# A convolution and state-space stack: the last projection through memory, the gate begun amid the last convolution, scans made up bit by bit, step sizes in one projection

## The chip, the cores and the metric

The kernel runs on one core of one Trainium2 chip. A core has five engines with a queue of instructions each: TensorE (PE in the profile, its weight loads PEld) multiplies matrices, VectorE (DVE) and ScalarE (ACT) work elementwise, GpSimd (POOL) does elementwise work too, and SyncE (SP) here only issues DMAs. An engine runs its queue in order; queues wait for each other by semaphores. Data lies in the chip's SBUF, results of matmuls in PSUM, everything larger in memory behind DMAs. The metric is the device time of one execution in microseconds (us); lower is better.

## The reference

Eight images of 256 channels and 32 x 32 places pass through four layers, each on the group norm `_gn` of its input and added to it:

```python
x = x + L0(_gn(x))   # attention, 8 heads of 64, queries and keys normalized to length 1, times 10
x = x + L1(_gn(x))   # 3x3 convolution 256 -> 256, weights = sign * scale
x = x + L2(_gn(x))   # 3x3 convolution 256 -> 256
x = x + L3(_gn(x))   # the mixer below
```

The mixer sees an image as 1024 places (N) of 256 channels:

```python
xn = layernorm(xs)                                   # over channels
for each of 4 blocks of 64 channels (mamba):
    u, z = split(xc @ inw.T); u = silu(conv4(u))     # 128 inner channels
    xdbc = u @ xpw.T                                 # 4 + 16 + 16 columns
    dt = softplus(xdbc[..., :4] @ dtw.T + dtb);  Bm, Cm = xdbc[..., 4:20], xdbc[..., 20:]
    h_t = exp(dt_t * A) * h_(t-1) + dt_t * u_t * Bm_t ;  y_t = sum over 16 states of h_t * Cm_t + u_t * D
    xm = (y * silu(z)) @ outw.T + skip * xc
Q = qpw(qdw(x_concat));  xg = sigmoid(Q) * xm        # one gate per block and place
R = rpw(rdw(xg)) + xg                                # depthwise 3, then 256 -> 256
xm2 = fpw(fdw(cat(xs, R))) + xs                      # depthwise 3, then 512 -> 256
x_out = cat(lc(xm2), mha(xm2)) @ fc_w.T + fc_b       # depthwise 3 beside attention, 8 heads of 32
xi = gelu(layernorm(x_out)); xi = ln_hw(xi); xi = dwc 3x3 (xi)
out = layernorm(xi) @ proj_w.T + proj_b
```

All of it is fp32.

## The kernel before

**Stages.** A tile framework orders the instructions: the program issues them as Python generators run, a scheduler orders each engine's queue by priority, data and free buffers, and sets the semaphores. Stage b of eight runs three images side by side: the scans of image b (`scan_layers`, L1028), and a dense stream (`dense`, inside the main loop at the end of the function) with the rest of the mixer of image b-1 and layers 0 to 2 of image b+1. Ahead of stage 0 stand layers 0 to 2 of image 0, after stage 7 the back of image 7. In stage 0 the dense stream has only a front, in stage 7 only a back; stages 1 to 6 have all three.

**Pace.** `interleave` (L1449) runs the dense stream step by step. Each step names its cost, about the microseconds of its matmuls; after each `pace` of cost the scans get one step of 149. `PACE` is 1.8 for stage 0, 2.95 for stages 1 to 6, 1.6 for stage 7. A dense stream with a lull gives a cost of 0 for some steps and pays what it owes with the next step (`lull`); `slow` takes a share of 0.35 of the front attention's cost. A scan instruction may not be moved ahead of the dense instruction issued before it on its engine (`Paced`, L97).

**Order of a dense stream.** In stages 1 to 6:

1. `back_layers` of b-1 (L1193): qdw and qpr (the gate: a convolution over 3 places and a 4 x 4 product as matmuls, tanh on ScalarE, two multiplications on VectorE), loads of xs (the mixer's input, kept in memory as xd), depthwise rd, projection rpw, depthwise fd (4 tiles), projection fpw, then `mixer_attention`: v, q/k, 64 units of scores, exp and values (tiles qk, p, acc; results o3), during which the depthwise `local` tiles and the next image's statistics are made (step 56).
2. `front_attention` of b+1 (L598): four double blocks of v (w<-xn matmuls), then `pair(0)`, the q and k of the first two heads with their lengths.
3. `back_out` of b-1 (L1356): the last projection of attention and local tiles, `fc`, 16 matmuls; two results xo go to memory.
4. The rest of `front_attention`: 64 units of two heads each, with sums by VectorE.
5. `front_convs` (L772): projection wout, group norm, convolution 1 (72 matmuls of 512 columns), group norm, convolution 2. Amid its steps, at the places (5, 6, 8 ... 26), stands `back_end` of b-1 (L1374): xo is loaded, layer norm with gelu, `ln_hw`, the 3x3 depthwise convolution (dw, 16 VectorE ops), layer norm, projection projw, and the output.

**Scans.** A branch (block of 64 channels) has its input prepared in `branch_front` (L806): minw, a convolution over 4 places on VectorE (u), projection mxpw to 36 rows, of which 32 (B and C) go to memory and the last 4, copied with them by ScalarE into `low`, give the step sizes dt in a second matmul with K = 4 (mdtw). dt and dt * u (du) go to memory and come back with each row on 4 groups of partitions. `scan_steps` (L907) then has 16 units a branch, 64 an image: GpSimd multiplies du and B ("drive", L958), ScalarE makes the decays (da), VectorE runs two scans, GpSimd multiplies with C ("weigh", L990), and two matmuls a unit, y<-hs,sel, add up the states. `branch_back` closes the branch with z and moutw.

**Buffers that matter.** `work` tiles are 12 buffers of 128 x 1026; PSUM has two `big` tiles of 128 x 1024, one `acc`, two `da`, one `y`. Loads of scans, stores and round trips through memory go by SP's queue, weights by ScalarE's.

Of the kernel before, what the change touches and what calls it, by code (L numbers as in the profile page):

```python
# [19 lines left out]
P = 128  # L20
# [13 lines left out]
def preact_stack(ctx: ExitStack, tc: tile.TileContext, I, out, cols):  # L34
# [130 lines left out]
    mdtw = wp.tile([36, NB, P], F32, name="mdtw")  # L165
    nc.sync.dma_start(out=mdtw[32:36], in_=I["mdtw"])
# [75 lines left out]
    for t in images + [raw]:  # L242
        nc.gpsimd.memset(t, 0.0)

# [353 lines left out]
    def front_attention(src, img, exact=False):  # L598
# [11 lines left out]
        for kt in range(0, NKT, 2):  # L610
            ps = big_tile()
            for i in range(2):
                for c in range(2):
                    tensor.matmul(
                        ps[:, HALVES[i]],
                        xn[c][:, (kt + i) * P : (kt + i + 1) * P],
                        wv[c],
                        start=c == 0,
                        stop=c == 1,
                    )  # L620
            vector.tensor_copy(
                v[:, kt : kt + 2].rearrange("p a b -> p (a b)"), ps
            )
            yield 3.4
# [98 lines left out]

        if exact:
            attention_exact(heads())
        else:
            first = pair(0)
            yield 3.4
# [77 lines left out]
    def branch_front(i, xn, br):  # L806
# [34 lines left out]
        for h in range(2):  # L841
            ps = da_tile()
            tensor.matmul(
                ps[0:36], mxpw[:, i], u[:, HALVES[h]], start=True, stop=True
            )
            scalar.copy(low[0:36, HALVES[h]], ps[0:36])
# [12 lines left out]
        for h in range(2):  # L859
            ps = da_tile()  # L860
            tensor.matmul(
                ps, mdtw[32:36, i], low[32:36, HALVES[h]], start=True, stop=True
# [330 lines left out]
    def back_layers(img, exact=False, begin=None):  # L1193
# [52 lines left out]
        for t in range(2):  # L1246
            depthwise3(rd[t][:, 0:N], xm[t], "rdw_w", "rdw_b", t)

# [28 lines left out]

        local = []
# [6 lines left out]
        for n, cost in enumerate(mixer_attention(x2, img, exact)):  # L1285
# [3 lines left out]
            if n == 56 and begin is not None:  # L1289
                next(begin)  # L1290
        while len(local) < 2:
            add_local()
        img["mix"] = local
# [62 lines left out]
    def back_out(img):  # L1356

        local, o = img.pop("mix"), img.pop("o3")
        img["xo"] = xdp.tile([2, P, N], F32, tag="xo", name="xo_d")

        def evac_fc(m, ps):
            xo = work("xo")[:, 0:N]
            scalar.activation(xo, ps, AF.Identity, bias=fc_b[:, m : m + 1])
            nc.sync.dma_start(out=img["xo"][m], in_=xo)

        srcs = [t[:, 0:N] for t in local + o]
# [7 lines left out]
    def back_end(img, out_b):  # L1374
        xo = [work("xo")[:, 0:N] for _ in range(2)]
        for t in range(2):
# [284 lines left out]
```

## Time and profile before

| | us |
|---|---|
| median of 8 runs | 6522.96 |
| lowest and highest | 6516.68, 6534.22 |
| the profiled execution: time | 6528.06 |
| its span, first to last instruction | 6526.2 |
| TensorE busy | 5561.0 |
| VectorE busy | 4008.6 |
| GpSimd busy | 2721.6 |
| ScalarE busy | 2714.1 |
| granted TensorE clock, mean | 0.91 |

The profile has several views: busy time of each engine in the span and in 40 slices, busy time in chosen stretches, instructions in order of time with what each waited for, and waits added up by who waited for whom. In the timeline a line is a run of equal instructions: start, length, engine, operation, output<-inputs, form and count, then in brackets the idle time before it and what ended it. A matmul of 512 columns stands there as two records. Times inside the span are counted from its first instruction. The stages begin at about 383, 1019, 1786, 2564, 3336, 4106, 4868 and 5640 us; the back of the last image begins at 6209.

### The profile page before, as it was taken

How to read it: one execution, taken by the hardware profiler on the slowest of the kernel's cores; microseconds unless marked ns; L12 is line 12 of the kernel's file. 1: busy time of each engine (PE TensorE's matmuls, PEld its weight loads, DVE VectorE, ACT ScalarE, POOL GpSimd, SP SyncE). 2: the span in 40 equal slices, each digit the busy share in tenths (PEclk: the TensorE clock that was granted, in tenths of full speed). 3: DMA queues.
4: the chain of work that ended last, by engine and by line, in shares of the span. 5: the costliest groups of instructions: out<-in, count | busy, mean ns of one | idle time of the engine just before them, and what ended most of it. 6: DMA issues, size and time to landing. Idle time of an engine off the chain costs nothing.

```text
span 6526.2 us, 52241 instructions
## 1 busy us (share of the span) xinstructions
PE 5561.0 (85%) x17310; PEld 1882.1 (29%) x17310; DVE 4008.6 (61%) x4612; ACT 2714.1 (42%) x3253; POOL 2721.6 (42%) x1302
## 2 busy tenths in 40 slices
PE   8887688998889978989889988899889997877496
PEld 2331133223332233222332233322332223311232
DVE  4248846577556775567755766567756677545622
ACT  3224424553255533544336442455325543345242
POOL 0007653634535243542526436353444535266600
PEclk9988899999899989999899998999899998988697
DMA  1023232322233122321223222232223312233201
GB/s 42 26 63 82 73 94 71 91 67 72 79 90 87 45 80 78 104 78 48 78 79 95 78 58 82 83 92 59 78 83 86 91 46 76 69 98 95 79 26 37
DMA packets 220145, 479.21 MB, mean 73 GB/s; under 512 B 60500, under 2 KB 102100, under 8 KB 218840
## 3 DMA queue, kind: packets, MB, share of 16 engines
q1 hardware_dynamic: 163416, 402.34, 21.8%
q10 hardware_dynamic: 56448, 73.43, 3.9%
q8 instruction: 139, 2.28, 0.2%
q14 instruction: 142, 1.16, 0.1%
HBM read 402.70 MB, written 64.49 MB: 72 GB/s over the span
## 4 chain that ended last, share of the span: by engine, by line
PE 49%; DVE 24%; ACT 7%; DMA 7%; issue 6%; POOL 5%; SPq 1%; ACTq 0%; DVEq 0%; POOLq 0%
PE big L105 30%; PE acc L105 11%; DVE hs L105 7%; PE da L105 6%; DVE p L105 4%; POOL hs L990 4%; PE y L105 3%; DVE dw L105 2%; ACT p L105 2%; ACT da L105 2%; DVE u L105 2%; DMA dt<-dt_m 1%; DVE dt L105 1%; POOL hs L958 1%; DMA bc<-bc 1%
## 5 line engine op out<-in xcount | busy, mean ns | idle before, releaser
L958 POOL TENSOR_TENSOR hs<-du,bc 128x1024 f32<-128x1024 f32 x512 | 1345.5, 2648 | 1620.7 <-DMA du<-du_m 1102.8
L990 POOL TENSOR_TENSOR hs<-hs,bc 128x1024 f32<-128x1024 f32 x512 | 1299.0, 2538 | 1004.6 <-DVE hs L105 846.0
L105 ACT ACTIVATE p<-big 128x1024 f32<-128x1024 f32 x1024 | 1038.9, 1021 | 734.1 <-PE big L105 725.7
L105 PE MATMUL acc<-p,v 128*64 128x512 f32 x4096 | 1153.5, 635 | 17.2 <-ACT o L105 12.2
L105 ACT ACTIVATE da<-dt,a_neg 128x512 f32<-128x512 f32 x1024 | 685.1, 687 | 1064.0 <-DVE hs L105 473.2
L105 PE MATMUL big<-im,w 128*128 128x512 f32 x2304 | 1108.3, 635 | 14.7 <-ACT im L105 14.7
L105 DVE TENSOR_TENSOR p<-p 128x1024 f32<-128x1024 f32 x448 | 769.6, 1718 | 261.1 <-PE acc L105 122.1
L105 DVE TENSOR_TENSOR_SCAN hs<-da,carry,hs 128x512 f32<-128x512 f32 x512 | 621.9, 1264 | 278.3 <-ACT da L105 201.4
L105 DVE TENSOR_TENSOR_SCAN hs<-da,hs 128x512 f32<-128x512 f32 x512 | 600.5, 1210 | 247.7 <-ACT da L105 238.5
L105 PE MATMUL y<-hs,sel 128*32 128x512 f32 x2048 | 459.7, 680 | 284.4 <-POOL hs L990 283.5
L105 PE MATMUL big<-q,k 64*128 64x512 f32 x2048 | 628.5, 670 | 63.3 <-ACT p L105 27.0
L105 PE MATMUL big<-qk,qk 64*128 64x512 f32 x2048 | 626.4, 659 | 53.3 <-ACT p L105 41.6
L105 PEld LDWEIGHTS big<-im,w 128*128 128x128 f32 x2304 | 451.0, 202 | 693.8 <-issue 642.9
L105 PEld LDWEIGHTS acc<-p,v 128*64 128x64 f32 x4096 | 214.7, 138 | 825.8 <-issue 730.5
L989 POOL COPY carry<-hs 128x2 f32<-128x2 f32 x256 | 87.5, 342 | 863.6 <-DVE hs L105 748.4
L105 PEld LDWEIGHTS big<-qk,qk 64*128 64x128 f32 x2048 | 172.0, 191 | 489.6 <-issue 285.6
L105 PEld LDWEIGHTS big<-q,k 64*128 64x128 f32 x2048 | 171.0, 192 | 489.6 <-issue 271.2
L105 PE MATMUL big<-xn,w 128*128 128x512 f32 x512 | 243.4, 631 | 28.0 <-DVE v L105 28.0
L105 DVE SCALAR_TENSOR_TENSOR dw<-xo,vec,dw 128x961 f32<-128x961 f32 (+1 forms) x128 | 243.2, 1945 | 29.6 <-ACT dw L105 29.1
L105 PEld LDWEIGHTS y<-hs,sel 128*32 128x32 f32 x2048 | 59.4, 113 | 594.0 <-POOL hs L990 438.9
L105 DVE SCALAR_TENSOR_TENSOR u<-raw,vec,u 128x1024 f32<-128x1024 f32 x96 | 162.4, 1691 | 84.9 <-ACT u L105 83.3
L105 PE MATMUL big<-o,w 128*128 128x512 f32 x384 | 181.2, 624 | 30.2 <-DVE o L105 30.2
(211 smaller groups left out, 5042.9 us busy)
## 6 DMA issues: line engine op xcount, KB each, us to landing
bc<-bc SPq DMA_DIRECT2D x1024, 128.0 KB
du<-du_m SPq DMA_DIRECT2D x512, 128.0 KB
dt<-dt_m SPq DMA_DIRECT2D x512, 128.0 KB
w<-in_wc ACTq DMA_DIRECT2D x192, 192.0 KB
rs<-inv SPq DMA_DIRECT2D x64, 256.0 KB
dt_m<-dt SPq DMA_DIRECT2D x64, 256.0 KB
du_m<-a SPq DMA_DIRECT2D x64, 256.0 KB
w<-in_wqk ACTq DMA_DIRECT2D x64, 128.0 KB
```

The lines of the kernel that those rows point to most:

```text
L105: made = issue(*args, **kwargs)
L958: nc.gpsimd.tensor_mul(u["hs"], u["du"], both_groups(u["bc"][:, 0]))
L989: nc.gpsimd.tensor_copy(carry[:, u["q"], g : g + 2], hs[:, :, HALF - 1])
L990: nc.gpsimd.tensor_mul(hs, hs, both_groups(u["bc"][:, 1]))
```

## The change

- **Last projection.** `back_layers` stores local and o3 (4 tiles of 512 KB) to memory at its end. `back_out` loads them and is no longer run before the front attention, but amid `front_convs`, after the wout projection's steps, ahead of `back_end`; its results xo stay in SBUF, so that their two stores and two loads go.
- **Front's start.** `pair(0)` is made after two of the four blocks of v.
- **Gate.** The first three steps of image b's own `back_layers` (`EARLY`: gate, and rd) run at the last places of stage b's `front_convs`, once the scans of image b are through; stage b+1 goes on from there. Stage 1 still begins its back afresh.
- **Scans.** `PACE` of stages 1 to 6 is 2.78 instead of 2.95. A lull's debt is paid with at most a quarter of each step's cost (`MAKE_UP`). With it the scans are issued to their end at a cost of 417 of 440 in a stage, where they ended with the last step before.
- **Step sizes.** At the start the two weights of the step sizes are multiplied into one of 128 x 128 a branch; dt comes from u in one matmul with K = 128. mxpw has 32 rows.

```diff
-    mdtw = wp.tile([36, NB, P], F32, name="mdtw")
-    nc.sync.dma_start(out=mdtw[32:36], in_=I["mdtw"])
+    mdtw = wp.tile([P, NB, P], F32, name="mdtw")
...
+    low_rank = work("low_rank")[0:DTR, 0:N].rearrange("r (k i n) -> r k i n", k=2, i=NB)
+    nc.sync.dma_start(out=low_rank[:, 0], in_=I["mxdt"])
+    nc.sync.dma_start(out=low_rank[:, 1], in_=I["mdtw"])
+    made = acc_tile()
+    for i in range(NB):
+        tensor.matmul(
+            made[:, i * P : (i + 1) * P],
+            low_rank[:, 0, i],
+            low_rank[:, 1, i],
+            start=True,
+            stop=True,
+        )
+    vector.tensor_scalar_mul(mdtw.rearrange("p i n -> p (i n)"), made, 0.5)
...
+        for kt in range(0, NKT, 2):
...
             yield 3.4
+            if kt == 2 and not exact:
+                first = pair(0)
+                yield 3.4
...
         else:
-            first = pair(0)
-            yield 3.4
             yield from attention(
...
-                ps[0:36], mxpw[:, i], u[:, HALVES[h]], start=True, stop=True
-            )
-            scalar.copy(low[0:36, HALVES[h]], ps[0:36])
+                ps[0 : 2 * DS], mxpw[:, i], u[:, HALVES[h]], start=True, stop=True
+            )
+            scalar.copy(low[0 : 2 * DS, HALVES[h]], ps[0 : 2 * DS])
...
-                ps, mdtw[32:36, i], low[32:36, HALVES[h]], start=True, stop=True
+                ps, mdtw[:, i], u[:, HALVES[h]], start=True, stop=True
...
             depthwise3(rd[t][:, 0:N], xm[t], "rdw_w", "rdw_b", t)
+        yield 0
...
+        img["mix"] = xdp.tile([4, P, N], F32, tag="mix", name="mix")
...
-            if n == 56 and begin is not None:
-                next(begin)
+            if n == 56 and "begin" in img:
+                next(img["begin"])
...
-        img["mix"] = local
+        for t, part in enumerate(local + img.pop("o3")):
+            nc.sync.dma_start(out=img["mix"][t], in_=part[:, 0:N])
...
-        local, o = img.pop("mix"), img.pop("o3")
-        img["xo"] = xdp.tile([2, P, N], F32, tag="xo", name="xo_d")
+        srcs = [work("mix")[:, 0:N] for _ in range(4)]
+        for t in range(4):
+            nc.sync.dma_start(out=srcs[t], in_=img["mix"][t])
+        yield 0
+        xo = img["xo"] = [work("xo")[:, 0:N] for _ in range(2)]

         def evac_fc(m, ps):
-            xo = work("xo")[:, 0:N]
-            scalar.activation(xo, ps, AF.Identity, bias=fc_b[:, m : m + 1])
-            nc.sync.dma_start(out=img["xo"][m], in_=xo)
-
-        srcs = [t[:, 0:N] for t in local + o]
+            scalar.activation(xo[m], ps, AF.Identity, bias=fc_b[:, m : m + 1])
...
-        xo = [work("xo")[:, 0:N] for _ in range(2)]
-        for t in range(2):
-            nc.sync.dma_start(out=xo[t], in_=img["xo"][t])
+        xo = img.pop("xo")
...
-                yield cost + owed
-                owed = 0.0
+                more = min(owed, MAKE_UP * cost)
+                owed -= more
+                yield cost + more
...
+    MAKE_UP = 0.25
+    PLACES = [1, 4, 4, 4, 4, 5, 6, 8, 9, 10, 11, 12, 13, 14, 15, 16]
+    PLACES += [18, 20, 22, 24, 26, 27, 28, 29]
+    EARLY = 3
-    PACE = [1.8] + [2.95] * (batch - 2) + [1.6]
+    PACE = [1.8] + [2.78] * (batch - 2) + [1.6]
...
-            for n, cost in enumerate(back_layers(last, begin=front)):
+            back, begun = last.pop("back", None), EARLY
+            if back is None:
+                back, begun = back_layers(last), 0
+            if front is not None:
+                last["begin"] = front
+            for n, cost in enumerate(back, begun):
                 yield cost
-                if n == 2 and front is not None:
+                if n == 3 and front is not None:
                     next(front)
+            ending = chain(back_out(last), back_end(last, out[b - 1]))
...
-            yield from islice(front, 4)
-            yield next(front)
-            yield from back_out(last)
+            yield from islice(front, 5)
             yield from slow(front)
+            imgs[b]["back"] = back_layers(imgs[b])
             yield from amid(
                 lull(front_convs(imgs[b + 1]), LULLS),
-                back_end(last, out[b - 1]),
-                (5, 6, 8, 9, 10, 11, 12, 13, 14, 15, 16, 18, 20, 22, 24, 26),
+                chain(ending, islice(imgs[b]["back"], EARLY)),
+                PLACES,
             )
```

## The prediction

> **What bounds the kernel now.** I read the page's busy shares and slices first, then the table of stages for one image, then TensorE's timeline and waits at the places where that table shows it idle. One profiled execution gives all durations. Its span is 6526.2 us and its time 6528.06, 5.1 us above the median 6522.96 of the eight runs, so the sum is made against 6528.06 and 5 us are taken off at the end. A difference under 0.2% (13 us) I count as no change.
>
> ```profile
> PE 5561.0 (85%) x17310; PEld 1882.1 (29%) x17310; DVE 4008.6 (61%) x4612; ACT 2714.1 (42%) x3253; POOL 2721.6 (42%) x1302
> PE   8887688998889978989889988899889997877496
> POOL 0007653634535243542526436353444535266600
> ```
>
> TensorE carries the span, at 85%; GpSimd, which drives and weighs the scans, falls to 2 or 3 tenths at each image's boundary. The steady stages (one image's back, the next one's front, a third one's scans) last 762 to 778 us. The stage from 4105 us, cut at its parts:
>
> ```profile
> 4105.00:4146.00 41.00, 31.00 (x101) 15.24 (x99) 30.06 (x73) 21.52 (x23) 0.00 (x0) 0.88 0.24 84
> 4183.00:4363.00 180.00, 165.56 (x628) 42.43 (x628) 102.78 (x95) 115.60 (x139) 113.43 (x58) 0.97 0.38 102
> 4396.00:4416.00 20.00, 16.58 (x48) 6.33 (x40) 16.35 (x25) 9.18 (x13) 5.70 (x3) 0.97 0.33 104
> 4416.00:4598.00 182.00, 172.50 (x628) 46.15 (x624) 140.34 (x140) 97.38 (x118) 61.46 (x24) 0.98 0.19 53
> 4621.00:4640.00 19.00, 13.52 (x50) 9.27 (x50) 15.30 (x33) 5.10 (x5) 7.17 (x4) 0.64 0.06 21
> 4640.00:4760.00 120.00, 95.86 (x220) 34.80 (x218) 97.86 (x101) 37.26 (x43) 65.41 (x29) 0.87 0.28 81
> ```
>
> Columns: length, then busy time of TensorE, its weight loads, VectorE, ScalarE and GpSimd, granted clock, DMA. The two attentions (lines 2 and 4) are TensorE's own time at nearly full clock. It loses at the boundaries: the back's start (line 1), after the first group norm's statistics (line 5, clock 0.64) and in the first convolution (line 6, VectorE 82% busy). Line 3 holds the last projection.
>
> ```profile
> 4386.30 9.39 PE L105 MATMUL big<-xn,w 128*128 128x512 f32 x16 [4.90 <-DVE v L105]
> 4396.62 7.13 PE L105 MATMUL big<-local,w 128*128 128x512 f32 x16
> 4403.59 7.03 PE L105 MATMUL big<-o,w 128*128 128x512 f32 x16
> 4415.03 1.92 PE L105 MATMUL y<-hs,sel 128*32 128x512 f32 x4 [3.42 <-POOL hs L990]
> 4416.88 1.76 PE L105 MATMUL big<-q,k 64*128 64x512 f32 x4
> 4624.57 0.39 PE L105 MATMUL acc<-mv,gmat 128*128 128x4 f32 x2 [3.44 <-DVE mv L105]
> 4627.36 6.99 PE L105 MATMUL acc<-mean_w,ln_sq 128*128 128x1 f32 x32
> 4639.45 7.40 PE L105 MATMUL big<-im,w 128*128 128x512 f32 x12
> ```
>
> A matmul of 512 columns is two records, 0.86 us. The last projection (32 records, 13.8 us) stands between the q/k projection and the front attention; from the last projection of attention to the first convolution matmul pass 18.3 us (4621.1 to 4639.4) with little to do.
>
> ```profile
> PE y L105 <- POOL hs L990: 30.6, 14, 4.4
> PE acc L105 <- DVE mv L105: 6.4, 2, 3.4
> ```
>
> The largest wait of this stage, 30.6 us in 14 pieces, is for weighed scan states; 19.4 us of it lie in 4640 to 4760, behind VectorE's depthwise convolution.
>
> **The change part by part**, in the order in which the changed program's engines hold their instructions.
>
> *Last projection out of the front's start.* Stages 1 to 6 each lose its 13.8 us there. From the back attention's last matmul group (4363.5) to the first score (4416.9) are 53.4 us. After the change: value blocks 0 and 1, q/k, value blocks 2 and 3, scores. The matmuls up to 4395.6 remain, with their 4.9 us wait (32 us). What is late next is the k chain: in image 0, where nothing covers it, 6.2 us pass between q/k and scores ("<-ACT k"). Two value blocks (6.9 us) now cover it, but VectorE copies them out behind the chain and one scan pair, about 3 us more. So 35.4 us, a gain of 18. Bounds: 20 (no wait) and 8 (copying the value blocks out holds the scores as long as the old projection's rest).
>
> *The projection behind the front's first group norm.* Its 13.8 us fill the 18.3 us there. It waits for its PSUM banks (two evacuations of 1.28 us with statistics between, about 2.5 us) and the statistics matmuls in its midst wait some 1.5 us; the scan matmuls and the step-size matmul (1.7 us) stay. The first convolution matmul comes about 3 us later than now. The layer norm's 32 small records, 7.0 us here at the low clock and 3.6 at full clock, move into the convolution: 3.6. Cost 6.6 instead of 13.8 + 3.6 = 17.4; bounds 0 and 17.4. On SP four stores of 512 KB replace two, and four loads two. The stores stand among scan loads near the back attention's end, the last behind the final multiplication of o3; behind it wait dt and bc loads, whose units have 6 to 23 us of slack there. The loads are issued where the two xo loads stand (4610.7); those two are read 7.8 and 9.9 us later, so at 2.1 us each the last of four lands at 4624.8, against a first use at 4621 and a last one 10 us after. Nothing, then; the cover gone, it would be the wait of the present xo reader, 14.4 us. At the end of the run the trip lies before the projection instead of after it (6.95 us from projection to squares now): 0, within 5 us.
>
> *First convolution.* VectorE gains the projection's time to work ahead on the scans, and the changed order puts three instead of four scan pairs inside the depthwise ops. I take 4 us of the 19.4 us of waits. Bounds: 15 gained, 9 lost (the eight units 40 to 47 now stand within 33 matmuls instead of 43: 8.6 us less cover). The made-up emission and pace 2.78 are in this: 20 units in the back attention, 28 in the convolutions, as before; the last one ends 18 instead of 8 matmuls before the end.
>
> *Gate amid the last convolution.* Now 79.9 us pass from the last convolution matmul (4103.9) to the back attention (4183.8), and the first scan matmul comes at 4217.6. The changed order leaves 48.6 us of TensorE work in that stretch, and it waits for VectorE's list (evacuation, three rd ops, eight fd ops of 1.28 us, two r, and the statistics chain threaded between: 25 us until all of fd is there), so about 64 us. But the scans' first step sizes come only some 4 us sooner (77.7 us after the convolution now): the attention runs into its first scan matmul about 6 us sooner than now with one or two units (2.07 us each) more done. Gain 9. The qdw and qpr matmuls (6.9 us) and two short waits for their ScalarE steps, 2 us, go into the convolution: loss 9. Net 0; bounds 7 gained, 9 lost. The two xs loads (512 KB each on SP) move with it to a place where the image's scan loads are all issued; the next image's input load (1 MB) comes one step later, some fifty steps before its statistics; the gate's tanh costs no table load more: the changed program has twelve table loads fewer (1.28 us each) in all, on ScalarE, whose 42% are covered.
>
> Against that move stands the dw row: 1193 to 3327 ns beside GpSimd, and 1209 to 1246 for the same 16 ops at the end of the run, where GpSimd is idle. The moved gate and rd ops follow the image's last weighing (4089.5 + 2.4, 12 us before the convolution's end), so I price them at 1.2 to 1.3 us as now.
>
> The Trainium skill (SBUF — State Buffer, "SBUF: two separate sides") says that a VectorE op with two SBUF inputs and a GpSimd op that reads SBUF exclude each other for a whole instruction. By the rule six moved ops beside GpSimd could wait one 2.35 us weighing each, 14 us a stage, and the sum would be 85 us higher; by the rows it stays.
>
> *Step sizes in one projection.* Same count of matmuls (da<-low,mdtw at 720 ns becomes 128 rows deep, like da<-u,w_mxpw at 698); they no longer wait for the two copies of low (1.4 us). That is in the 4 us above. Four small matmuls and two small loads at the start: 0 to 1 us.
>
> *Pair 0 before the last value blocks* also helps where no projection lies between: image 0 waits 6.2 us and stage 0 4.1. I take 8 of those 10. Stage 7 (GpSimd busy 312 of 469 us, TensorE clock 0.76) goes at the scans' pace and gains about the 4 us of their earlier start.
>
> Sum: six stages of -18 + 6.6 - 4 + 0 = -15.4 are -92; with -8, -4 and 1 it is -103; 6528 - 103 = 6425, and less 5 us **6420 us**.
>
> **Rivals.**
> *A, the scan waits grow (slower).* In the first convolution VectorE is the limit: each scan pair queues behind three depthwise ops, and each of TensorE's y waits there takes 2.3 to 4.4 us. If denser scans double the 30.6 us, six stages pay 184 and the time is 6604; growth of 17 us a stage decides, and at 24 it is 6564. For it: the slack of 0.1 us of most units there. Against it: fewer scan pairs inside the depthwise ops.
> *B, the projection hides nothing new.* If scores wait for the value copies and the projection pays its full 13.8 us (+10.8 a stage), 6485. For it: VectorE 15.3 of 19 us busy in the new place. Against it: most of those are 0.2 us ops of a chain that TensorE waits out.
> *C, the boundaries go wholly.* Gate -7, first convolution -15 and front start -20 a stage in place of 0, -4 and -18: 120 us more, 6300. For it: 11 us of VectorE work leave the boundary. Against it: the first scan matmul.
>
> **How the numbers follow.** Forecast 0.53 (its own range 6345 to 6495), A 0.18, B 0.14, C 0.15. The range 6305 to 6550 leaves out half of C's lower side and A's upper half. Faster by over 0.2%: forecast, C and most of B, 0.79; the seams of B and A give 0.06 for no change; slower 0.15.
>
> **What the profile after would show.** Right: 35 instead of 53 us between the attentions with value blocks before scores; mix matmuls under the first group norm with a clock above 0.64; y waits of about 27 us a stage; the back attention beginning some 64 us after the convolution. Wrong: mix loads in TensorE's waits, a y wait of 5 us or more at the back attention's first scan matmul, or y waits above 47 us a stage.

## The result, and the profile after

The changed kernel takes 6550.19 us, the median of 13 runs (6538.53 to 6565.80), beside 6524.97 for the kernel before in 36 runs: a ratio of 1.0039 (95% interval 1.0031 to 1.0047). It is slower by 0.4%, where 6420 us and "faster" were forecast. Its profiled execution took 6539.92 us (span 6538.2), some 10 us under its median, where that of before stood 3 us over the median of its 36 runs; so the profiles show only 12 of the 25 us.

The page's busy shares after:

```profile
PE 5502.2 (84%) x17318; PEld 1848.5 (28%) x17318; DVE 4001.3 (61%) x4613; ACT 2701.1 (41%) x3241; POOL 2733.7 (42%) x1302
```

TensorE is busy for 59 us less than before, in a span that is 12 us longer. The stage that the prediction showed, after the change, cut at its parts (columns as in the prediction: length, TensorE, its weight loads, VectorE, ScalarE, GpSimd, clock, DMA):

```profile
4094.80:4155.40 60.60, 53.70 (x169) 27.84 (x168) 42.30 (x83) 20.89 (x24) 0.00 (x0) 0.94 0.17 57
4155.40:4351.20 195.80, 176.31 (x633) 45.24 (x632) 108.77 (x104) 122.92 (x147) 117.54 (x60) 0.91 0.38 103
...
4568.60:4617.20 48.60, 42.55 (x114) 16.01 (x112) 32.44 (x45) 16.27 (x19) 13.28 (x8) 0.96 0.34 102
4617.20:4723.40 106.20, 85.49 (x244) 35.61 (x240) 93.18 (x83) 31.31 (x37) 63.60 (x26) 0.92 0.31 87
...
4739.20:4862.90 123.70, 113.35 (x305) 44.41 (x304) 59.77 (x71) 34.66 (x44) 62.64 (x33) 0.93 0.27 80
sum 768.10, PE 675.88 PEld 227.30 DVE 505.20 ACT 337.14 POOL 343.86; mean PE 84.48 PEld 28.41 DVE 63.15 ACT 42.14 POOL 42.98
```

The rows are: from the last convolution to the back attention, that attention, the way to the first convolution, the first convolution, and the second. Left out are the front attention with the way to it, and the 15.8 us between the convolutions; the sum has all parts. The last row of the same view of before, cut at the same places:

```profile
sum 762.80, PE 678.45 PEld 229.78 DVE 508.46 ACT 338.88 POOL 340.21; mean PE 84.81 PEld 28.72 DVE 63.56 ACT 42.36 POOL 42.53
```

TensorE is idle for 92.2 us of this stage (768.10 less 675.88), where it was idle for 84.4; in the mean of stages 2 to 6 it is 91.8 where it was 86.9. The change was to fill idle time; it moved it, and added some. The means of stages 2 to 6, read from TensorE's records:

| part (us) | before | forecast | after |
|---|---|---|---|
| last convolution to back attention | 81.9 | 64 | 60.6 |
| back attention | 182.5 | 191 | 195.6 |
| to the front attention | 53.0 | 35 | 35.1 |
| front attention | 183.5 | 183.5 | 182.0 |
| to the first convolution | 40.9 | 44 | 48.8 |
| first convolution | 110.2 | 110 | 105.9 |
| to the second | 13.4 | 13 | 15.8 |
| second convolution | 105.3 | 114 | 123.7 |
| stage | 770.7 | 755 | 767.4 |

(The forecast column is the prediction's terms laid on the first column.) Outside these stages: image 0's layers took 10.3 us less, stage 0 16.7 more, stage 1 3.2 more, stage 7 up to the last attention 13.4 more, the rest 3.4 more. With the 16.4 us that stages 2 to 6 win together, that is the 10 us by which TensorE's last matmul comes later.

The largest waits of TensorE in this stage after, and two lines of the same view of before:

```profile
PE y L105 <- POOL hs L1006: 31.0, 11, 10.0
PE big L105 <- ACT p L105: 19.2, 7, 9.2
PE big L105 <- ACT big L105: 11.9, 4, 6.1
```

```profile
PE big L105 <- ACT p L105: 5.6, 5, 2.9
PE big L105 <- ACT big L105: 2.1, 3, 1.3
```

The waits for weighed scan states have not grown (30.6 before) in the steady stages; in stage 7 they have, from 69.5 to 101.1. The waits for ScalarE have: for exps from 5.6 to 19.2 us, for the squares of q and k from 2.1 to 11.9. The longest of each, first ScalarE in the back attention, then TensorE between the attentions:

```profile
4187.37 1.30 ACT L105 ACTIVATE da<-dt,a_neg 128x512 f32<-128x512 f32 x2 [4.15 <-DMA dt<-dt_m]
...
4193.39 1.92 ACT L105 ACTIVATE p<-big 128x1024 f32<-128x1024 f32 x2
```

```profile
4358.64 3.70 PE L105 MATMUL big<-w,xn 128*128 128x512 f32 x8
4362.18 7.16 PE L105 MATMUL big<-xn,w 128*128 128x512 f32 x16
4375.41 6.22 PE L105 MATMUL big<-w,xn 128*128 128x512 f32 x8 [6.07 <-ACT big L105]
```

On ScalarE the decays of a scan unit (da) wait for step sizes that are still on their way through memory, then unit by unit for the scans, and the attention's exps (p), issued behind them, begin only at 4193.39: 9.2 us of TensorE. In the second place the squares of q and k stand behind two decays that start at 4373.03, and hold the PSUM tile that the third value block wants.

### The profile page after: what moved, and what is told of

It is laid out like the page before. It is cut to its first block, busy times and chain, and to the rows that moved or that the text cites. A ratio compares the mean times of both kernels' runs of the same rounds, so it can differ in the third digit from the quotient of the medians.

```text
span 6538.2 us, 52259 instructions
## 1 busy us (share of the span) xinstructions
PE 5502.2 (84%) x17318; PEld 1848.5 (28%) x17318; DVE 4001.3 (61%) x4613; ACT 2701.1 (41%) x3241; POOL 2733.7 (42%) x1302
## 4 chain that ended last, share of the span: by engine, by line
PE 53%; DVE 23%; issue 6%; ACT 6%; DMA 6%; POOL 4%; SPq 1%; ACTq 0%; DVEq 0%; POOLq 0%
PE big L105 33%; PE acc L105 12%; DVE hs L105 6%; PE da L105 5%; DVE p L105 4%; DVE dw L105 3%; POOL hs L1006 3%; PE y L105 3%; DVE u L105 2%; DVE t L105 1%; POOL hs L974 1%; DMA du_m<-a 1%; ACT p L105 1%; DMA dt<-dt_m 1%; ACT da L105 1%
## 5 line engine op out<-in xcount | busy, mean ns | idle before, releaser
L105 PE MATMUL big<-im,w 128*128 128x512 f32 x2304 | 1090.9, 625 | 20.4 <-ACT im L105 20.4
L105 DVE TENSOR_TENSOR p<-p 128x1024 f32<-128x1024 f32 x448 | 718.3, 1603 | 301.6 <-ACT p L105 204.5
L105 PE MATMUL big<-qk,qk 64*128 64x512 f32 x2048 | 652.7, 668 | 96.7 <-ACT p L105 87.1
L1005 POOL COPY carry<-hs 128x2 f32<-128x2 f32 x256 | 103.7, 405 | 831.2 <-DVE hs L105 756.8
L105 DVE SCALAR_TENSOR_TENSOR dw<-xo,vec,dw 128x961 f32<-128x961 f32 (+1 forms) x128 | 247.8, 1971 | 16.4 <-ACT dw L105 15.2
L105 PE MATMUL big<-xn,w 128*128 128x512 f32 x512 | 230.1, 601 | 0.0
L105 DVE SCALAR_TENSOR_TENSOR u<-raw,vec,u 128x1024 f32<-128x1024 f32 x96 | 139.8, 1456 | 85.3 <-ACT u L105 83.6
L105 PE MATMUL da<-xn,w_minw 64*128 64x512 f32 x256 | 157.0, 732 | 18.5 <-DVE shift L105 10.3
```

Of the source, the lines that this page charges most:

```text
L105: made = issue(*args, **kwargs)
L1005: nc.gpsimd.tensor_copy(carry[:, u["q"], g : g + 2], hs[:, :, HALF - 1])
```

## The experiments

Ratios are to the kernel before, timed in the same runs, with 95% intervals. Three kernels, whose output is not the reference's, were run once and have one time only.

### The gate late, and the old pace

```diff
-    EARLY = 3
+    EARLY = 0
```

> The changed kernel with the gate back at the start of the next stage (EARLY 0), all else as changed. Theory G (the early gate lets the back attention overtake the scan front: ScalarE then holds exps behind decays that wait for the step sizes' loads): in stages 2 to 6 the back attention starts some 82 us after the convolution instead of 61, lasts 183 instead of 196 us, and the last convolution takes 105 to 110 instead of 124; the stage gets some 10 us shorter, the kernel about 50 us faster than the changed one, near 6500. Theory P (the denser pace does it, as stage 1 has the longer attention without an early gate): the attention stays at 194 to 198, only 7 to 9 us leave the last convolution against 21 us at the start, the stage gets about 12 us longer, the kernel near 6610.

The second kernel has that edit and, in `lull` and `PACE`, what stood there before the change:

```diff
-    PACE = [1.8] + [2.78] * (batch - 2) + [1.6]
+    PACE = [1.8] + [2.95] * (batch - 2) + [1.6]
...
-                more = min(owed, MAKE_UP * cost)
-                owed -= more
-                yield cost + more
+                yield cost + owed
+                owed = 0.0
```

> As the run before, and also pace 2.95 with a lull's debt paid at once, as before the change. Theory G: within 10 us of the run before it (about 6500), attention 183. Theory P: the attention falls from about 196 to 183 us in stages 1 to 6, so some 80 us under the run before it. Both leave projection through memory, the front's start and the one-projection step sizes in place: the stage from attention's end to front attention stays 35 us.

Gate late: 6501.56 us, 0.9974 (0.9964 to 0.9984), so 0.65% faster than the changed kernel: the early gate costs some 42 us. That is the time that Theory G gave (near 6500), but not for its reason, so by luck. With the gate late the back attention still takes 197.7 us (mean of stages 2 to 6), and the start 73.0, not 82. With the old pace too: 6536.12 us, 1.0025 (1.0014 to 1.0036), the attention 182.9, the start 81.2, the first convolution 127.0 instead of 109.3. Theory G expected this kernel within 10 us of the gate-late one, Theory P some 80 under it; it is 35 over it. The row of the back attention, gate late and then with the old pace:

```profile
4162.20:4357.10 194.90, 171.98 (x628) 43.51 (x628) 108.50 (x100) 118.76 (x143) 127.10 (x64) 0.95 0.36 97
```

```profile
4179.80:4361.90 182.10, 169.14 (x628) 42.91 (x628) 102.15 (x94) 115.21 (x139) 113.94 (x59) 0.95 0.39 107
```

So the longer attention comes with the new pacing, pace and debts together (Theory P was right on that, wrong on the gate), and so do 8 of the 21 us that the start lost, since the image's scans are through sooner. The gate's own part is the difference of the changed kernel and the gate-late one: 12.4 us less at the start, 2.1 less in the back attention; 9.5 more before the first convolution, 3.4 less in it, 5.9 less behind it, 16.2 more in the second convolution, where the two gate matmul groups take 7.4: 4 us a stage lost. Stage 7 takes 651.9 us instead of 640.7.

The kernel with the gate late and the old pace also shows what became of the front's saving. The first convolution in the kernel before, then in this one:

```profile
4639.30:4748.50 109.20, 89.79 (x209) 33.21 (x208) 91.11 (x80) 33.79 (x39) 60.98 (x27) 0.89 0.29 84
```

```profile
4613.60:4741.30 127.70, 102.83 (x257) 39.93 (x255) 100.03 (x94) 40.73 (x48) 65.30 (x31) 0.87 0.28 81
```

In the means of stages 2 to 6 the way to the front attention is 19.0 us shorter than before and that attention 9.0; the way to the first convolution is 1.4 us longer, that convolution 16.8, the way to the second 2.6, the second 6.3. The stage takes 769.4 us instead of 770.7. Of the first convolution's 16.8 us, 12.7 are matmuls that stand there now and 4.0 more idle time. The idle time that the moved projection fills (8.9 us before the first convolution, now 3.7) comes back between the convolutions (4.9, now 13.6), where only 8 matmul records are left of 16.

### The last two images handed over directly

```diff
+        mixed = local + img.pop("o3")
+        if img.get("keep"):
+            img["mix"] = mixed
+            return
...
+        if img.get("keep"):
+            srcs = [t[:, 0:N] for t in img.pop("mix")]
+        else:
```

> The changed kernel, but images 6 and 7 hand local and o3 to the last projection in SBUF, without stores and loads. Theory M (in stage 7 nothing covers the trip, TensorE waits 29 us for it and scan matmuls queue behind): the wait for mix goes, stage 7 falls from 652 to 630 to 640 us and the end after the last attention from 109 to 104 to 106; the kernel 15 to 25 us faster than the changed one. Rival S (scans set stage 7's end): stage 7 stays at 648 to 652 and only the 3 to 5 us of the end are won.

6527.79 us, 1.0019 (1.0010 to 1.0029), 13 us under the changed kernel by the ratios, 22 by the medians. TensorE's largest waits in stage 7, of the changed kernel and of this one:

```profile
PE y L105 <- POOL hs L1006: 101.1, 26, 19.0
PE big L105 <- DMA mix<-mix: 29.1, 1, 29.1
```

```profile
PE y L105 <- POOL hs L1006: 99.3, 29, 19.7
...
PE big L105 <- DVE o L105: 16.6, 1, 16.6
```

The 29.1 us for the trip are gone; 16.6 of them come back as the wait for the last attention results (14.2 in the kernel before). Stage 7 falls by 6.8 us to 645.1, the rest from 245.9 to 235.6. Theory M holds in its mechanism; stage 7 gave less than expected (630 to 640 us) and the end more.

### The first pair late in stage 0

```diff
-            if kt == 2 and not exact:
+            if kt == (6 if img.get("late") else 2) and not exact:
...
+    imgs[1]["late"] = True
```

> The changed kernel, but in stage 0 alone the q and k of the front's first pair are made after all value blocks, as before. Theory Q (made early they stand ahead of the scan front on ScalarE, and stage 0 goes at the scans' pace): the first drive comes about 90 us after the stage's start instead of 100.5, stage 0 takes 637 us instead of 654, the kernel is about 17 us faster than the changed one. Rival D (the deeper step-size matmul or the earlier start itself does it): stage 0 stays within 5 us of 654.

Stage 0 takes 637.0 us, to a tenth what it took before, and GpSimd's first drive comes 88.3 us after its start instead of 100.5 (88.3 before the change). ScalarE there, in the changed kernel and in this one, between the copy of the convolution's input (raw) and its first product (u):

```profile
421.00 0.57 ACT L105 COPY raw<-da 128x512 f32<-128x512 f32 x1
...
429.56 1.15 ACT L105 ACTIVATE k<-k,ss 128x1024 f32<-128x1024 f32 x1 [3.61 <-DVE ss L105]
...
430.62 1.23 ACT L105 ACTIVATE u<-raw,vec 128x1024 f32<-128x1024 f32 x1
```

```profile
422.90 0.59 ACT L105 COPY raw<-da 128x512 f32<-128x512 f32 x1 [0.73 <-PE da L105]
423.52 1.24 ACT L105 ACTIVATE u<-raw,vec 128x1024 f32<-128x1024 f32 x1
```

Theory Q is shown for the stage: the squares and the scaling of k hold the scan's u for 9 us. The whole kernel, 6538.24 us and 1.0043 (1.0028 to 1.0058) in five runs, does not show the gain; its profiled execution ends 15 us sooner than the changed kernel's.

### The three mends together

> Three changes to the changed kernel at once: gate late (EARLY 0), images 6 and 7 handed over in SBUF, and q and k of the first pair after all value blocks in stage 0. If the three effects stand in different stages and add up (48 us from the gate, 17 to 22 from the direct hand-over, 12 to 17 from stage 0), the time is 6460 to 6470 and some 0.9% under the kernel before. If they overlap (an earlier stage only makes a later one wait), it stays at 6485 to 6500.

6463.63 us, 0.9916 (0.9896 to 0.9935), inside the range expected if the effects add up. By the medians they do: 49, 22 and 12 us alone, 87 together. By the ratios the three alone come to some 52 us (42, 13 and 3 lost) and together to 80: the direct hand-over wins more behind the last convolution with the gate late (28.9 us in the profiles) than with it early (17.2). Without these three costs the change is 0.8% faster than the kernel before.

### Without the depthwise convolution's VectorE work

Both leave out these 16 operations an image:

```diff
-                vector.scalar_tensor_tensor(
-                    acc[:, rows, at],
-                    src[:, from_rows, from_at],
...
-                )
```

> The kernel before without the 16 VectorE operations an image of the 3x3 depthwise convolution (only its middle place is left): the computation is not the reference's. It is the base of the next run. VectorE loses some 30 us an image inside the first convolution; if VectorE's queue holds the scans there, TensorE's y waits in the first convolution fall from 21 to under 10 us and the stage shortens by 12 or more; if not, by under 5.

> The changed kernel with the gate late and the old pace, again without the 16 VectorE operations an image of the depthwise convolution (the computation is not the reference's): against the run before it only the projection's way, pair 0 and the step sizes differ. Theory V (the depthwise operations on VectorE give back in the first convolution what the front saves): without them the front's 28 us stay won, the first convolution is within 5 us of the run before it, and a stage is 12 or more us shorter than there. Rival S (the scan chain's own rate gives it back): the first convolution is again 12 to 18 us longer than in the run before it, and a stage is within 4 us of it.

One run each: 6392.42 and 6420.43 us. Stages 2 to 6 take 755 us in the first and 754 in the second; the 28 us between the two lie in stages 0 and 7, which lose as in the changed kernel (16.7 and 13.9). VectorE's load did cost the kernel before some 16 us a stage in the first convolution (110 to 94, its y waits 20.9 to 10.9, where under 10 were expected); but the front's 28 us (19 on the way to the front attention, 9 in it) are given back without it too: the first convolution takes 117 us against 94, the second 114 against 105. Theory V falls. Rival S has the stage right (within 4 us) and the first convolution too short (12 to 18 us longer, 23 came); that the scans' own rate gives the 28 us back is not shown by it. Of the 23 us TensorE is busy for 15.8 and idle for 7.0, so most of it is work that stood elsewhere. At the old pace the projection's way, pair 0 and the step sizes bring a steady stage nothing, whatever VectorE does in the convolution.

### The kernel before with the new pace alone

```diff
-                yield cost + owed
-                owed = 0.0
+                more = min(owed, MAKE_UP * cost)
+                owed -= more
+                yield cost + more
...
-    PACE = [1.8] + [2.95] * (batch - 2) + [1.6]
+    PACE = [1.8] + [2.78] * (batch - 2) + [1.6]
```

> The kernel before with only the pace 2.78 and the debts of a lull paid bit by bit. Theory C (the scans' work costs TensorE the same wherever it is put; the new pace moves it from the first convolution into the back attention): the back attention takes 195 to 199 us instead of 183, the start 72 to 75 instead of 82, the first convolution 92 to 97 instead of 110, and the stages stay within 5 us of before: 6490 to 6530. Rival H (the pace alone is the gain of the gate-late kernel, and projection and pair 0 bring nothing): 6490 or less. Rival N (the pace needs the shorter front): slower than 6540.

6636.72 us, 1.0176 (1.0159 to 1.0193): slower than any theory but N had it. The attention is 197 us as expected, but the convolutions get no shorter (114.5 and 111). A stage takes 789 us. Theory C's reason fails too: the back attention holds 630 matmul records, with 20 scan units, in both kernels. The same work takes 14.6 us longer there, 8.0 of it idle time.

### Step sizes without the trip through memory

In the gate-late kernel the step sizes dt, and dt * u with them, are loaded from a tile in memory (`still`) that is written once, with zeros; the stores and the number and size of the loads stay, but no load waits for a store.

```diff
-                src = br[name][:, u["h"], g : g + 2].rearrange("d g n -> d (g n)")
+                src = still[:, u["h"], g : g + 2].rearrange("d g n -> d (g n)")
```

> The gate-late kernel, but dt and du are loaded from a copy in memory written once at the start (zeros, so the computation is not the reference's); the stores of dt and du and the loads' number and size stay, only the loads wait for no store. Theory T (at pace 2.78 the loads of dt come late and ScalarE holds the exps of the back attention behind the decays that wait for them): ScalarE's wait for dt (7.3 us in the back attention) goes, the back attention falls from 198 us to 183 to 188, a stage gets 8 to 15 us shorter. Rival W (more scan work on TensorE and ScalarE lengthens the attention, whatever it waits for): it stays at 194 to 199.

One run: 6401.2 us, its profile 111 us under that of the gate-late kernel. ScalarE's wait in the back attention of the gate-late kernel, which is not in that of this one, and what follows it on VectorE and TensorE:

```profile
4231.20 0.69 ACT L105 ACTIVATE da<-dt,a_neg 128x512 f32<-128x512 f32 x1 [7.26 <-DMA dt<-dt_m]
```

```profile
4232.00 2.46 DVE L105 TENSOR_TENSOR_SCAN hs<-da,carry,hs 128x512 f32<-128x512 f32 x2 [10.31 <-ACT da L105]
```

```profile
4237.04 2.08 PE L105 MATMUL big<-qk,qk 64*128 64x512 f32 x4 [5.16 <-ACT qk L105]
```

The back attention takes 186.7 us instead of 197.7 (means of stages 2 to 6), the stage 752.6 instead of 763.6; stage 0, with pair 0 early, 637.2 instead of 653.9. Theory T holds in its size: without the trip through memory 11 of the 15 us go by which this attention is longer than at the old pace. Its mechanism does not hold here. TensorE's waits for exps are as long in both (5.9 to 7.1 us with the trip and 4.9 to 8.3 without, in three stages); what goes is the 5.2 us in which the next scores wait for the copies of q and k (qk), since VectorE's copies stand behind two scans that the late decays hold. Nor does such a wait alone make the attention long: at pace 2.70, below, ScalarE waits 6.7 us for these loads, and the attention takes 187 us. The first drive of stage 0 comes 76.0 us after its start here, 12 us sooner than with pair 0 late, and the stage is no shorter for it: at 637 us the first drive no longer sets it.

### Step sizes with K = 4 again

The kernel with the three mends, with `mdtw` of 36 rows, `low` copied with its 36 rows and the matmul on `low[32:36]`, as before the change.

> The kernel with the three mends (gate late, images 6 and 7 direct, pair 0 late in stage 0), with the step sizes made by way of low and K = 4 again, as before the change. Theory 0 (one projection for the step sizes moves nothing): within 0.15% of the kernel with the three mends, 0.990 to 0.993 of before. Rival D (the scan front is on the path that sets a stage): 1.4 us or more of each stage, 10 to 20 us slower, 0.9935 to 0.9955.

6488.14 us, 0.9949 (0.9933 to 0.9964) against 0.9916 (0.9896 to 0.9935): 0.3%, some 22 us, with intervals that overlap by a little. A stage is 7.4 us longer in the mean of stages 1 to 6: the start 2.6 (75.9 and 73.3), the way to the first convolution 2.4, the second convolution 2.2. Rival D is the nearer.

### Other paces

Only the number changes, in the kernel with the three mends:

> The kernel with the three mends at pace 2.86 instead of 2.78. If the pace trades the back attention (198 us at 2.78, 183 at 2.95) against the first convolution (109 and 127) evenly, the time lies between: 0.992 to 0.997 of before. If there is a best place between, under 0.990.

> The kernel with the three mends at pace 2.70. If 2.78 is near the best: 0.992 to 1.000 of before, with a back attention over 198 us. If denser scans go on relieving the convolutions: under 0.990.

> The three mends at pace 2.90. If the time follows the density of the scans, it lies between 2.86 (0.9853) and the old pace (about 0.996 by the gate-late run at 2.95 less the two other mends), 0.986 to 0.993. If it follows where single scan steps fall (2.70, 2.78 and 2.86 gave back attentions of 187, 198 and 178 us, in no order), it may leave that on either side: under 0.985 or over 0.995, with a back attention unlike its neighbours' 178 and 183.

2.86: 6428.12 us, 0.9853 (0.9828 to 0.9878). 2.70: 6497.91, 0.9963 (0.9953 to 0.9974). 2.90: 6382.94, 0.9781 (0.9764 to 0.9797). The back attention takes 187, 198, 178 and 178 us at 2.70, 2.78, 2.86 and 2.90: it does not follow the density of the scans, and the units in it are 20 at each pace but 2.70, where they are 22. At 2.70 the time came where it was expected if 2.78 is near the best pace (0.992 to 1.000), which 2.78 is not. At 2.90 the time is under the 0.985 that was to speak for single scan steps; the attention was then to differ from that at 2.86, and it does not.

### The early gate at another pace

```diff
-    EARLY = 0
+    EARLY = 3
```

> The two other mends (images 6 and 7 direct, pair 0 late in stage 0) with the gate early, at pace 2.70; only the gate differs from the kernel with the three mends at 2.70 (0.9963 of before). Theory G (the early gate itself costs, at any pace: its matmuls and the scan waits it adds in the last convolution outweigh the start): 4 to 8 us a stage slower than that kernel, 1.000 to 1.005 of before; the start 61 to 63 us instead of 74, the last convolution 12 to 20 us longer. Theory L (at 2.78 it was where the scan steps fell): within 0.15% of it or faster, 0.990 to 0.998.

The gate's steps must come after the image's last scan, which a higher pace number puts later, so 2.70 was taken. 6533.11 us, 1.0016 (1.0006 to 1.0026), against 0.9963: the early gate costs 0.53%, 35 us, inside Theory G's range; the profiles show 19 of them. Here the start wins 15.6 us (74.0 to 58.4) and the back attention loses 21 (186.7 to 207.9), as the first Theory G had said of 2.78, where it was not so. ScalarE waits in it for the loads of dt for 9.0 us. The second convolution is 6.6 us longer and the way to it 9.4, where 12 to 20 in the last convolution were expected.

### The kernel before at other paces

> The kernel before with pace 2.86 and the debts of a lull paid bit by bit. Theory F (the projection's way and the front's start are what the good pace lets through): 0.995 to 1.010 of before, so 1 to 2.5% behind the kernel with the three mends at the same pace. Rival H (the pace is the whole gain, the moved work brings nothing): 0.985 to 0.991.

> The kernel before, with its pace 2.95, and only the debts of a lull paid bit by bit. Theory M (the debts paid at once after a lull, not the pace, are what costs the kernel before): 0.978 to 0.988 of before. Rival P (the pace 2.86 does it): 0.995 to 1.005. With neither the fall of single scan steps is what counts, and it may be anywhere between 0.985 and 1.02.

> The kernel before at pace 2.90 with the debts paid bit by bit; it stands beside the three mends at 2.90 (0.9781) as 2.86 does (0.9779 of before against 0.9853). If density sets the time: 0.975 to 0.985, near 2.86. If single steps do: over 0.990 or under 0.975, as 2.78 (1.0176) and 2.86 (0.9779) lie 4% apart.

2.86: 6381.47 us, 0.9779 (0.9763 to 0.9796). Debts bit by bit at 2.95: 6436.12, 0.9871 (0.9843 to 0.9900). 2.90: 6415.72, 0.9841 (0.9813 to 0.9869). The first is beyond Rival H's range (0.985 to 0.991) and far from Theory F's: two numbers of the change alone give the kernel before 2.2%, more than half of it by the debts, as Theory M of the second run has it. The third lies where density was to put it (0.975 to 0.985), and not where single steps were.

| pace | order of before | changed order, three mends |
|---|---|---|
| 2.95, debts at once | 1 | 1.0025 (gate late only) |
| 2.95, bit by bit | 0.9871 | |
| 2.90 | 0.9841 | 0.9781 |
| 2.86 | 0.9779 | 0.9853 |
| 2.78 | 1.0176 | 0.9916 |
| 2.70 | | 0.9963 |

The columns cross twice. At 2.78 the changed order gains 2.6%, at 2.86 it loses 0.8%, at 2.90 it gains 0.6%. What makes the same program 4% slower at 2.78 than at 2.86, in one stage (waits of TensorE, then the sums by stretch; first 2.78, then 2.86):

```profile
PE y L105 <- POOL hs L990: 30.3, 11, 5.5
PE big L105 <- ACT p L105: 14.7, 9, 8.3
```

```profile
PE y L105 <- POOL hs L990: 22.9, 8, 7.1
...
PE big L105 <- ACT p L105: 5.0, 4, 2.9
```

```profile
sum 792.00, PE 690.77 PEld 235.54 DVE 491.08 ACT 337.22 POOL 333.03; mean PE 86.35 PEld 29.44 DVE 61.38 ACT 42.15 POOL 41.63
```

```profile
sum 750.90, PE 670.69 PEld 228.81 DVE 483.40 ACT 337.67 POOL 343.16; mean PE 83.84 PEld 28.60 DVE 60.43 ACT 42.21 POOL 42.90
```

These two waits are 17.1 us longer at 2.78; others go both ways (for the squares of q and k 4.1 us at 2.78 and 10.7 at 2.86). Idle time differs by 21 us (101.2 and 80.2), and busy time by 20.

### The best version

The kernel before at pace 2.86 with two parts of the change, the step sizes in one projection and pair 0 early for image 0 alone.

> The kernel before at pace 2.86 with two parts of the change that showed gains: the step sizes in one projection and, for image 0 alone, q and k of the first pair ahead of the last value blocks. If their gains (20 us and 10 us) add to it: 0.973 to 0.976 of before, 6350 to 6370. If the step sizes gained only by where they put the scan steps at 2.78: 0.976 to 0.979.

```profile
PE 5440.1 (86%) x17318; PEld 1861.2 (29%) x17318; DVE 3894.8 (61%) x4613; ACT 2705.7 (43%) x3241; POOL 2735.0 (43%) x1302
```

6354.29 us, 0.9747 (0.9718 to 0.9775): the fastest, 2.5% under the kernel before and 2.9% under the changed one (0.9747 / 1.0039). Its profiled span is 31.4 us under that at 2.86 alone: 9 us before stage 0 and some 3 to 4 a stage, inside the range expected if the two gains add. They do not lie where they lay at 2.78: the back attention is 3.7 us shorter (177.3 and 181.0 in the mean of stages 2 to 6), the start and the way to the first convolution are shorter by 0.2 and 0.4. TensorE is busy for 121 us less than before.

## Why the prediction was wrong

**The step that failed** is that the sum takes the scans as a fixed small term, and with it the saving of the front as kept. It stands in the part on the first convolution: "The made-up emission and pace 2.78 are in this: 20 units in the back attention, 28 in the convolutions, as before", taken with 4 us of gain a stage and bounds of 15 gained and 9 lost. The number of units is as it said (20 and 28, before and after). What they cost is not. At the old pace the front saves its 28 us, and the first convolution alone takes 16.8 of them back, beyond the 9; the stage wins 1.3 us. In the changed kernel that convolution is 4.3 us shorter, near the forecast, but by luck: the back attention is 13.1 longer, the way to the first convolution 7.9 and the second convolution 18.4, where some 9, 3 and 9 were forecast. The new pacing, for its part, makes a stage of the kernel before 17.8 us longer (788.5), and one of the changed order with the gate late 5.8 shorter (763.6 from 769.4). On the whole kernel before, pacing is worth between 143 us gained (at 2.86) and 111 lost (at 2.78), more than all other terms. Against the kernel before at 2.78 the changed kernel is 1.3% faster (1.0039 / 1.0176), some 87 us, which is near the 79 us that the other terms summed to. That is no proof of these terms: their worth changes sign with the pace, so a sum over them had no fixed value.

That the kernel came out slower at all is the work of three other terms: the gate (0 in the sum, a cost of 35 to 42 us), stage 7 (4 gained, 13.4 lost) and stage 0 (some 3 gained, its share of the 8 for pair 0; 16.7 lost). With the three mended it is 62 us under the kernel before in the same runs, where 103 were forecast.

**Front's start**: 53 to 35.4 forecast, 53.0 to 35.1 measured, value blocks before the scores. The wait that took the old one's place was ScalarE's squares (6.1 us), not VectorE's copies: right in the number, with another cause.

**Projection behind the group norm**: the clock there is 0.96 instead of 0.80 in the mean, the loads show in no wait of stages 1 to 6, and the way to the convolution is 1.6 us shorter with the gate late, 1.4 longer with the old pace too, against the 3 forecast. The 7.9 after came with the early gate. What was left out is stage 7, which has no first group norm to hide the trip: "Stage 7 ... goes at the scans' pace and gains about the 4 us" lost 13.4, with 29.1 us of wait for mix. The sign "mix loads in TensorE's waits" was named as one against it, and came. At the end of the run 3.4 us were lost, within the bounds; against the direct hand-over the trip costs 10.3 there (245.9 and 235.6).

**Gate**: start and back attention together were to win 9 us and won 8.2 (264.4 to 256.2), but 8 us of the start's gain was the pace's. In the second convolution 9 us were priced and 18.4 came. The forecast named a y wait at the back attention's first scan matmul as the sign of a bad start; the late step sizes came as exps behind decays instead. The net is a cost of 35 to 42 us in the whole kernel, at two paces, where 0 was set with a bound of 9 a stage. Of the 16.2 us that the second convolution pays for it, 7.4 are the gate's matmuls, some 5 scan matmuls that came later in the stage (72 records instead of 56), and 3.8 idle time, nearly all of it y waits.

The row price of the moved VectorE operations held: rd took 1280 ns before and 1278 after. GpSimd's last weighing of the image ended at 4835.4 us and the gate's first VectorE operation began at 4857.3, so the rule in the Trainium skill (SBUF — State Buffer, "SBUF: two separate sides") on such operations beside GpSimd was not put to the test here; the 14 us a stage by it did not come.

**Step sizes**: put at 1.4 us within other terms; 2.6 us at the start, 2.4 before the first convolution and 2.2 in the second, 22 us in all at 2.78.

**Pair 0 early**: image 0 won 10.3 us, more than the 6.2 of its wait. Stage 0 was to win some of its 4.1 us of wait and lost 16.7: the step took TensorE's wait for the price, and did not ask what else stands on ScalarE behind the moved squares in a stage that goes at the scans' pace.

**Rivals.** A, the one that had the kernel slower, fell by its mechanism: y waits did not grow in the steady stages. It was also the only one to name the denser scans, and as y waits alone; B and C named the moved parts. The range's upper end, 6550, was 0.2 us short of the median. Of the signs of a right forecast three came (35.1 us between the attentions, the mix matmuls at a clock of 0.96, the back attention 60.6 us after the convolution), and the stage won 3.3 us instead of 15.4: each looked at one part, and the time went elsewhere.

What stays open: why 2.86 suits the one order and 2.90 the other, and what sets the rate at which the scans' work comes back in the convolutions. That single steps decide, and not density, is argued from times that go up and down with the pace and from attentions of 178 to 198 us with the same 20 units; the kernel before at 2.90 came where density would have it. Only at 2.78 was one such step (the wait for the trip) taken away, and the attention got 11 us shorter.

## What to carry to other kernels

Where a second stream of work is woven in by a pace, the pace is to be tried anew for each order before the order is judged: here the order of before and the changed order with its mends, each at its best pace tried, end within 2 us (6381 and 6383), and comparing them at one pace gives anything from 2.6% gained to 0.8% lost. When a part of a stage gets shorter, add up the whole stage: here 28 us won in the front stood again in the convolutions. When work is moved ahead on one engine, list what stands behind it on every queue that it issues to, above all in the first and last stages, where the other stream sets the end and the usual cover is missing. Idle time that a move fills is won only if what the later work waits for comes earlier too.

## What the runs showed of the hardware

TensorE's busy time is not fixed by its matmuls. The kernel before has the same 17310 matmuls at both paces, but in one stage they are busy for 690.8 us at 2.78 and 670.7 at 2.86; over the run 5584.0 and 5462.3, with a mean granted clock of 0.898 and 0.911. Half of the 41 us between these two stages is busy time, beside the idle time. This was not in the prediction's prices, which took a matmul's length as it stood. More idle time does not always go with it: the changed kernel is idle for 1036 us where the kernel before is for 965, and busy for 5502.2 instead of 5561.0, at 0.911 and 0.910. Why is not shown.
